# Sorted expert tiles of layer 2: per-expert sets from one table, outputs two tiles behind, finer steps for routing and return

## The chip, the cores and the metric

The kernel runs on one core of a Trainium2 chip. The core has five engines that each work through their own instructions in order: TensorE (PE, matrix products; its weight loads are shown apart as PEld), VectorE (DVE), ScalarE (ACT), GpSimd (POOL) and SyncE (SP, which here only starts transfers). Transfers between the main memory (DRAM) and the on-chip memory are moved by 16 DMA engines; SP, ACT and POOL start them. The metric is the device time of one execution in microseconds, lower is better.

## The reference, cut to what matters

The program is a network of four layers on x[2, 1024, 128]. Each layer adds half a feed-forward part (FFN), an attention, and the same half FFN again:

```
x = x + 0.5 * L2_ffn(layernorm(x));  x = x + L2_attn(x);  x = x + 0.5 * L2_ffn(layernorm(x))
```

Layer 0 has a mixture of 6 experts and a latent attention, layer 1 an FFN that selects columns by an argmax and a compressed, selected and windowed attention, layer 3 a mixture of 8 experts with a small attention in front of it, and between its two FFN parts a gated recurrence (minGRU). Layer 2's FFN is what the change is about. It has 8 experts, and each token uses two of them:

```
logits = x @ router_w                      # [tokens, 8]
gate_vals, gate_idx = top_k(logits, 2);  gate_w = softmax(gate_vals)
h   = gelu(x @ w1[e] + b1[e])              # 128 -> 512
out = h @ w2[e] + b2[e]                    # 512 -> 128
res = x + out
y   = (res - mean(res)) / sqrt(var(res) + 1e-6) * gamma[e] + beta[e]
result = sum over the token's two experts of gate_w * y
```

w1, b1, w2, b2, gamma and beta all belong to the expert. Layer 2's attention has 16 heads of 64, with a norm per head on queries and keys, and a tanh clamp on the scores. Everything is in 32-bit floats.

## The kernel before, in words

x stays on the chip as 16 tiles of 128 tokens; four of them make a quarter q (512 tokens). Work that belongs to another part of the program is cut into pieces and kept in threads: `Ctx.later` (L68) adds a thread, `Ctx.tick` (L71) advances the first `width` threads by one stretch each, up to the next `None`, and `Ctx.need` runs a thread to its end. A main loop calls `tick` once or twice per step, so the pieces land between its own instructions. PE's order is exactly the order of the program text so made. A scheduler orders the other engines, and each engine's queue is in order.

**Layer 2's FFN** (`l2_ffn`, L1316) computes only the two chosen experts of a token, by sorting. It is run twice, before and after layer 2's attention, each time for two halves of 1024 tokens.

- `l2_ffn_prep` (L1196), per quarter: layernorm (`norm_pieces`, transposed by L166), the normed rows stored to DRAM (xd), router (L222), gates and the part of beta (L247, L266, L273).
- `l2_route` (L1223), per half: counts the tokens of each expert with small products (L1246 to L1252), places them (DVE), builds one-hot rows (r_b L1293, r_a) and inverts the list with 16 products (L1303). The result: for each of 23 tiles of 128 sorted rows the token numbers (r_tok) and the tile's expert (r_exi), and for each token where its two rows lie (r_si).
- `l2_ffn` then goes through the tiles in groups of 4 (the last has 3), 46 tiles for two halves. `fetch` gathers a tile's rows (xg, L1331, on POOL), loads its expert number into a register on PE, ACT, DVE and SP (L1332), and starts the transfer of the expert's w1 (256 KB, L1340). `turn` (L1361) transposes a group's rows and copies them out of the accumulator banks as xgT. `hidden` is four products (L1375) and four gelus (L1383), whose bias is picked from a table by the register. `output` is a product of ones with b2 in three bf16 parts (L1393) and four products with w2 (L1402), one tile behind `hidden`. `combine`, per group, adds xg (L1421), takes mean and variance, multiplies by gamma (L1427) and stores the rows to DRAM (yd, L1431). Hidden products of two tiles share one pair of banks. One tick comes with every second tile.
- `l2_back` (L1454), per half, after the half's last store: 16 gathers of 128 rows (yg, L1465), all issued in the first tick of its thread, then for each quarter the scaling and the addition into x (L1470 to L1477).
- `l2_expert_weights` (L1176) loads w2 (2 MB), gamma, and b2, which `three_parts` splits on DVE into three bf16 parts (tag l2f_b, L370). It is called before the second l1_ffn and again near the attention's end.

**Around it.** `l1_ffn` (L679; its second call is the one right before the first tiles) goes through 16 tiles t with one tick each; its steps are L689, L690 (a copy on ACT), L696, L705, L712. `l2_attn` (L1489) goes through 8 groups of four heads. `project` makes a group's queries, keys and values as eight products (L1516, L1520; squares on POOL L1529) and eight turns (L1538, L1542, L1545). The first projection is done in one go before the loop; the others are spread over the 16 steps of the group before. A step has scores (L1586), tanh and exp (L1593, L1594) and mix (L1619). Near its end the last group ticks twice per step. Layer 3's FFN uses `experts` (L280): per quarter eight steps of a hidden product (L290) and an output (L308), with a tick of width 3 per step. Its two calls are named "j" and "k"; in their ticks run layer 3's attention and its norms (xn, nn, zn by L156, L158 and L166; L1737 pq; at; L1784 pp), and after each quarter of "j" the recurrence (xa, L1871, y L1896).

Of the kernel before, what the change touches and what calls it, by code (L numbers as in the profile page):

```python
# [279 lines left out]
def experts(c, pool, rs, w1, w2, b1, func, n, hc, combine, key, b2=None, width=2):  # L280
# [20 lines left out]
    def output(q, e, hT):  # L301
        py = c.long("py").rearrange("p (j d) -> p j d", j=4)
        if b2 is not None:
            rows = b2[:, e * P : (e + 1) * P].unsqueeze(1).to_broadcast([3, 4, P])
            nc.tensor.matmul(py, lhsT=c.ones16[0:3, :], rhs=rows, start=True, stop=False, skip_group_check=True)
        for j in range(4):
            for k in range(hc):
# [4 lines left out]
                    start=(k == 0 and b2 is None),  # L312
                    stop=(k == hc - 1),
                    skip_group_check=b2 is not None,
                )
        return combine(q, e, py)

    last, due = None, deque([[]])

    def step(q=None, e=None):  # L320


        nonlocal last
        now = None if q is None else (q, e, hidden(q, e))
        if last is not None:
            for k, piece in enumerate(output(*last)):
                while len(due) < k + 2:
                    due.append([])
                due[k + 1].append(piece)
        last = now  # L330
        for piece in due.popleft():
            piece()
        if not due:
            due.append([])
        c.tick(width)

    for q in range(NC):
        c.need((key, q))
        for e in range(n):
            step(q, e)  # L340
    step()
    while any(due):
        for piece in due.popleft():
            piece()


def add_gated(c, rs, tile_of, n, done):


    def combine(q, e, py):  # L350
# [5 lines left out]
        return []  # L356
# [322 lines left out]
def l1_ffn(c, w, rs, key, done):  # L679
    nc = c.nc  # L680
    with c.pool("l1f", 2) as pool:
# [54 lines left out]
        for t in range(NT + 5):  # L736
# [4 lines left out]
            if t < NT:  # L741
                av[t] = choose(t)
                if t % 4 == 2 and t // 4 < 3:
                    latent(t // 4 + 1)
            if 0 <= t - 4 < NT:
                aT[t - 4] = output(t - 4, av.pop(t - 4)[1])
            if 0 <= t - 5 < NT:
# [399 lines left out]
def l2_consts(c, pool):  # L1147
    w = {n: c.load(pool, f"l2f_{n}") for n in "router b1 beta".split()}
# [23 lines left out]
def l2_attn_weights(c, pool):  # L1172
    return {n: c.load(pool, f"l2a_{n}") for n in "wq wkv wo norm gq gk".split()}


def l2_expert_weights(c, pool, work):  # L1176
    w = {"w2": c.load(pool, "l2f_w2")}
    w["gamma"] = pool.tile([P, 8, P], F32, tag="l2f_gamma", name="l2f_gamma")
    c.nc.sync.dma_start(
# [964 lines left out]
```

## Time and profile before

| | us |
|---|---|
| median of 13 runs | 3162.29 |
| lowest, highest | 3155.42, 3168.08 |
| profiled execution | 3163.22 |
| span of its trace | 3161.5 |
| mean granted clock of PE | 0.93 |
| PE busy | 2737.2 |
| DVE busy | 2047.7 |

The stages that matter lie in the span as follows. The second l1_ffn runs from 1598.6 to 1685; the first tiles from 1707.06 (their first hidden product) to 1865.7 (last output); layer 2's attention from 1915.96 (first scores) to about 2670; the second tiles from 2687.06 to 2846.86; layer 3 from there to 3161.5.

| window | length | PE busy | DVE busy |
|---|---|---|---|
| second l1_ffn 1599 to 1685 | 86 | 74.93 | 68.61 |
| seam 1685 to 1707 | 22 | 5.46 | 11.78 |
| tiles 1707 to 1768 | 61 | 55.70 | 22.12 |
| first projection 1866 to 1916 | 50 | 21.83 | 33.27 |
| seam 2670 to 2687 | 17 | 2.30 | 10.86 |
| seam 2846 to 2858 | 12 | 3.63 | 7.86 |
| layer 3, 2858 to 2960 | 102 | 95.67 | 83.22 |
| layer 3, 2960 to 3162 | 202 | 181.00 | 123.72 |

How to read the profile: an idle time belongs to the instruction that stands behind it, and the name after the arrow is what released it. Idle time counts only on an engine that the end waits for, which here is mostly PE. A wait for several things is put down to the one that came last by the profile; "issue" means that nothing in the profile explains it. The 40 slices are 79 us each; digits are tenths. The matmul counts of a line in the timeline can be twice those of the code.

### The profile page before, as it was taken

Reading aid. Unit: us, or ns where it says so; the run is one execution under the profiler, and the core shown is the slowest. Engines: PE = TensorE matmul, PEld = TensorE weight load, DVE = VectorE, ACT = ScalarE, POOL = GpSimd, SP = SyncE. Lnnn points to the kernel's source line nnn. Section 1 sums busy time; section 2 is a strip of 40 time slices with the busy share of each in tenths; the row PEclk is TensorE's granted clock in tenths of the full one; section 3 lists DMA queues with packets and bytes.
Section 4 is the critical chain, followed back from the end, with each engine's and each line's share of the span. In section 5 each row is a group of like instructions: output and inputs, shape, how many; then the busy total and the mean of one; then the engine's idle time right before and its main releaser. Section 6 shows DMA issues by size and latency. Waiting matters only on the chain.

```text
span 3161.5 us, 44643 instructions
## 1 busy us (share of the span) xinstructions
PE 2737.2 (87%) x15214; PEld 1563.5 (49%) x15214; DVE 2047.7 (65%) x6398; ACT 1586.2 (50%) x3148; POOL 908.9 (29%) x861
## 2 busy tenths in 40 slices
PE   7899999999898877878876857999989996778989
PEld 5544545444565554444445743333333433776666
DVE  4666556655547768768575358777777786357874
ACT  3355455455433336566523425776766774344543
POOL 0011111111003445444343334443444442332110
PEclk9999999999999759999987879999999998889999
DMA  3000000000000000000013420000000011430000
GB/s 83 1 1 1 1 1 1 1 1 1 12 15 1 1 1 1 1 1 1 28 37 91 112 65 2 1 1 1 1 7 1 1 64 37 112 103 17 1 4 11
DMA packets 48990, 64.87 MB, mean 21 GB/s; under 512 B 9924, under 2 KB 31701, under 8 KB 48124
## 3 DMA queue, kind: packets, MB, share of 16 engines
q1 hardware_dynamic: 38328, 48.74, 5.1%
q0 software_dynamic: 4992, 10.27, 1.7%
q10 hardware_dynamic: 5444, 3.01, 0.4%
q8 instruction: 122, 2.00, 0.3%
q14 instruction: 104, 0.85, 0.1%
HBM read 52.77 MB, written 9.22 MB: 20 GB/s over the span
## 4 chain that ended last, share of the span: by engine, by line
PE 65%; DVE 20%; ACT 5%; issue 4%; POOL 3%; DMA 2%; ACTq 0%; SPq 0%; DVEq 0%; POOLq 0%
PE ps L1586 6%; PE po L1619 6%; PE ph L290 5%; PE ps L492 5%; PE py L308 5%; PE po L534 5%; PE ptp L520 4%; PE ph L1375 3%; PE pr L472 3%; PE py L1402 2%; PE po L1071 2%; PE pt L1059 2%; PE pr L562 1%; PE pqk L1520 1%; ACT pe L1037 1%
## 5 line engine op out<-in xcount | busy, mean ns | idle before, releaser
L1593 ACT ACTIVATE pe<-ps 128x1024 f32<-128x1024 f32 x256 | 249.0, 1021 | 181.7 <-PE ps L1586 129.1
L1586 PE MATMUL ps<-tr 64*128 64x512 f32 x1024 | 269.5, 647 | 1.6 <-ACT pe L1593 1.6
L1619 PE MATMUL po<-pe,v 128*64 128x512 f32 x1024 | 249.9, 609 | 3.7 <-ACT pe L1594 3.7
L505 ACT ACTIVATE pe<-ps,nm 128x512 f32<-128x512 f32 (+3 forms) x384 | 219.3, 577 | 64.3 <-DVE nm L503 60.4
L1594 ACT ACTIVATE pe<-pe 128x2048 f32<-128x2048 f32 x128 | 244.7, 1911 | 4.0
L503 DVE TENSOR_REDUCE nm<-ps 128x2 f32<-128x256 f32 (+1 forms) x192 | 182.6, 951 | 95.1 <-PE ps L501 61.4
L353 DVE SCALAR_TENSOR_TENSOR x<-py,gates,x 128x128 f32<-128x128 f32 x448 | 132.8, 343 | 161.7 <-PE py L308 161.6
L99 ACT COPY pT<-ptp 128x512 f32<-128x512 f32 x192 | 91.9, 479 | 252.2 <-PE ptp L520 252.2
L492 PE MATMUL ps<-kT,qT 64*128 64x512 f32 (+3 forms) x768 | 177.4, 538 | 30.0 <-ACT pe L505 11.4
L1383 ACT ACTIVATE hT<-ph,l2f_b 128x128 f32<-128x128 f32 x368 | 111.4, 366 | 171.0 <-PE ph L1375 161.2
L534 PE MATMUL po<-pT,v 128*64 128x512 f32 (+3 forms) x768 | 166.8, 513 | 0.0
L520 PE MATMUL ptp<-ident,pe 128*128 128x128 f32 x1152 | 162.5, 277 | 0.2 <-ACT rb L570 0.2
L1375 PE MATMUL ph<-xgT,w 128*128 128x128 f32 x736 | 112.7, 301 | 55.2 <-issue 39.6
L1586 PEld LDWEIGHTS ps<-tr 64*128 64x128 f32 x1024 | 92.7, 195 | 125.8 <-issue 90.9
L1619 PEld LDWEIGHTS po<-pe,v 128*64 128x64 f32 x1024 | 62.7, 138 | 179.9 <-issue 152.9
L520 PEld LDWEIGHTS ptp<-ident,pe 128*128 128x128 f32 x1152 | 123.1, 141 | 52.3 <-issue 40.4
L308 PEld LDWEIGHTS py<-l3f_w,hT 128*128 128x128 f32 x1024 | 125.7, 194 | 32.6 <-issue 30.5
L1331 POOL DMA_INDIRECT xg<-xd,r_tok x92 | 87.2, 948 | 189.2 <-issue 95.9
L1606 POOL TENSOR_TENSOR acp<-pe 128x1024 f32<-128x1024 f32 x32 | 76.8, 2401 | 223.3 <-ACT pe L1594 132.9
L1529 POOL TENSOR_TENSOR sq<-raw 128x512 f32<-128x512 f32 x64 | 89.5, 1398 | 164.3 <-DVE raw L1527 107.0
L475 POOL TENSOR_TENSOR qT<-tab 128x512 f32<-128x512 f32 x32 | 40.6, 1269 | 329.4 <-DVE tab L474 184.0
L1045 POOL TENSOR_SCALAR pe<-pe,rs 128x256 f32<-128x256 f32 (+7 forms) x128 | 94.3, 749 | 141.8 <-DVE rs L1042 76.8
(426 smaller groups left out, 6380.7 us busy)
## 6 DMA issues: line engine op xcount, KB each, us to landing
w<-in_l2f_w SPq DMA_DIRECT2D x92, 256.0 KB, 3.4
yd<-y SPq DMA_DIRECT2D x20, 258.0 KB, 3.8
l2f_w<-in_l2f_w SPq DMA_DIRECT2D x2, 2048.0 KB, 8.6
xd<-xn SPq DMA_DIRECT2D x8, 256.0 KB, 2.3
l3f_w<-in_l3f_w SPq DMA_DIRECT2D x2, 1024.0 KB, 4.9
l0f_W<-in_l0f_W SPq DMA_DIRECT2D x2, 768.0 KB, 5.1
xg<-xd,r_tok POOLq DMA_INDIRECT x92, 3.4
l2a_wkv<-in_l2a_wkv SPq DMA_DIRECT2D x1, 1024.0 KB, 5.7
```

The lines of the kernel that those rows point to most:

```text
L290: nc.tensor.matmul(ph[:, a, :], lhsT=w1[:, e, (k + a) * P : (k + a + 1) * P], rhs=rs[q]["xT"], start=True, stop=True)
L308: nc.tensor.matmul(py[:, j, :], lhsT=hT[:, k, j * P : (j + 1) * P], rhs=w2[:, e, k, :], start=(k == 0 and b2 is None), stop=(k == hc - 1), ...
L492: nc.tensor.matmul(ps[:, h, :W], lhsT=u["qT"][r, q0 : q0 + P], rhs=u["kT"][r, gk * 512 : gk * 512 + W], start=True, stop=not diag,)
L503: nc.vector.tensor_reduce(nm, ps[:, :, :W], AX.X, ALU.max, negate=True)
L505: nc.scalar.activation(u["pe", n][:, h, i, :W], ps[:, h, :W], AF.Exp, bias=nm[:, h : h + 1], accum_out=u["rs"][:, n, i, h : h + 1],)
L520: nc.tensor.transpose(pt[:, i * P : (i + 1) * P], u["pe", n][:, h, i, j * P : (j + 1) * P], c.ident)
L534: nc.tensor.matmul(u["po", n][r, lo * P :], lhsT=u["v"][:, BLOCKS[n][1] * 4 + j, cols], rhs=u["pT", n, j][h][:, lo * P :], start=(j == 0), ...
L1375: nc.tensor.matmul(ph[:, a * P : (a + 1) * P], lhsT=wt[:, a * P : (a + 1) * P], rhs=xT[n][:, j * P : (j + 1) * P], start=True, stop=True,)
L1586: nc.tensor.matmul(ps[:, h, :], lhsT=tr[r, 1, p, k * P : (k + 1) * P], rhs=tr[r, 0, p, q * 512 : (q + 1) * 512], start=True, stop=True,)
L1593: nc.scalar.activation(pe[:, j], ps, AF.Tanh, scale=1.0 / 50.0)
L1594: nc.scalar.activation(pe, pe, AF.Exp, scale=50.0 * 0.125)
L1619: nc.tensor.matmul(u["po"][r, :], lhsT=u["v"][:, k, 2 * u["p"] + h, :], rhs=pe[:, j, h, :], start=(k == 0), stop=(k == TB - 1),)
```

## The change

One table in DRAM, `sets[128, 8, 772]`, holds for each expert w1 (512 columns), b1 (4), b2 (128) and gamma (128), the last two repeated on all 128 rows. Four transfers write it when the kernel starts. A tile now fetches two stretches of it: w1 with b1 (264 KB) and b2 with gamma (131 KB), up to six tiles ahead; registers are loaded once per group, on SP and on PE alone. The gelus' bias and the combine's gamma come from the tile's set, and b2 is added on DVE in the combine instead of by a product on PE. `l2_expert_weights` and both calls of `three_parts` are gone.

Outputs come two tiles behind the hidden products (hT has four buffers). A tick comes with every tile, and from tile 12 on two. A half's route is queued right after its gates, and half 0's first gathers and fetches are the tail of its route thread. `l2_back` issues its gathers in four steps with pauses of ticks, and the additions come some ticks after the gathers they need. The attention becomes a class whose first projection runs as thread pieces, so that it falls among half 1's tiles.

The numbers of ticks change: the second l1_ffn has three per t (one before), the last attention group four per step from step 10 on (two before), layer 3's "j" three per step for the first two quarters and two after (one before), "k" two (one before). Ticks now stand on both sides of an output product.

```diff
@@ experts
+            now = (q, e, hidden(q, e))
+            if ticks(q) > 1:
+                c.tick(width)
+            if last is not None:
+                output(*last)
+            if ticks(q) > 2:
+                c.tick(width)
+            last = now
+            c.tick(width)
@@ l1_ffn
+            if ticks > 1:
+                c.tick()
             if 0 <= t - 4 < NT:
                 aT[t - 4] = output(t - 4, av.pop(t - 4)[1])
+            if ticks > 2:
+                c.tick()
@@
-def l2_expert_weights(c, pool, work):
-    w = {"w2": c.load(pool, "l2f_w2")}
...
-    three_parts(c, work, c.load(work, "l2f_b2", rows=3), w["b2"])
+def l2_sets(c, dpool):
+
+    t = dpool.tile([P, 8, 772], F32, tag="sets", name="sets")
+    for cols, src in (
+        (slice(0, 512), c.dram["l2f_w1"]),
+        (slice(512, 516), c.dram["l2f_b1"].rearrange("p (e k) -> p e k", k=4)),
+        (slice(516, 644), c.dram["l2f_b2"].rearrange("o (e d) -> o e d", d=P).to_broadcast([P, 8, P])),
+        (slice(644, 772), c.dram["l2f_gamma"].rearrange("o (e d) -> o e d", d=P).to_broadcast([P, 8, P])),
+    ):
+        c.nc.sync.dma_start(out=t[:, :, cols], in_=src)
+    return t
@@ l2_ffn_prep
-    return [begin] + norm[:i] + [store] + norm[i:] + gates + [end]
+    return [begin] + norm[:i] + [store] + norm[i:] + gates[:1] + [chosen] + gates[1:]
@@ class L2Experts
+        halves[0]["then"] = [self.gather, self.fetch, self.fetch, None, self.gather] + [self.fetch] * 2
...
+    def fetch(self):
+
+        k = self.fetched
+        n, j = self.tiles[k]
+        if j == 0:
+            self.register[n] = self.load(n, ("SP",))
+        t = self.set[k] = {}
+        for name, cols, bufs in (("w1b1", slice(0, 516), 7), ("b2g", slice(516, 772), 10)):
+            t[name] = self.pool.tile([P, cols.stop - cols.start], F32, tag=name, name=name, bufs=bufs)
+            src = self.sets[:, bass.ds(self.register[n][j], 1), cols].rearrange("p e f -> p (e f)")
+            self.nc.sync.dma_start(out=t[name], in_=src)
+        self.fetched += 1
...
+        while self.gathered < min(self.tiles[k][0] + 3, len(self.groups)) and self.routed(self.gathered):
+            self.gather()
+        while self.fetched < min(k + 6, len(self.tiles)) and self.routed(self.tiles[self.fetched][0]):
+            self.fetch()
...
+                for a in range(4):
+                    b1 = t[:, 512 + a : 513 + a]
+                    nc.scalar.activation(hT[:, a, :], ph[:, a * P : (a + 1) * P], AF.Gelu, bias=b1)
...
+                nc.vector.tensor_add(res[:, 0:m, :], py[:, 0:m, :], self.xg[n][:, 0:m, :])
+                sets = [self.set.pop(k + j)["b2g"] for j in range(m)]
+                for j in range(m):
+                    nc.vector.tensor_add(res[:, j, :], res[:, j, :], sets[j][:, 0:P])
...
+            for k, (n, j) in enumerate(tiles):
+                self.ahead(k)
+                if k == 0:
+                    turn(0)
+                queue.append((k, n, j, hidden(k, n, j)))
+                c.tick()
+                if len(queue) > 2:
+                    output(*queue.popleft())
+                if j == 2 and n + 1 < len(groups):
+                    if n + 1 == self.gathered:
+                        self.ahead(k + 1)
+                    turn(n + 1)
+                if k >= 12:
+                    c.tick()
@@ l2_back
-    return [partial(fetch, 0), partial(fetch, 1), None, None, None, partial(add, 0), None, partial(add, 1), None]
+    pieces = [None] * 5
+    for piece in (partial(fetch, 0, 0), partial(fetch, 0, 1), partial(fetch, 1, 0)):
+        pieces += [piece, None, None, None]
+    return pieces + [partial(add, 0), partial(fetch, 1, 1)] + [None] * 5 + [partial(add, 1), None]
@@ class L2Attention
+    def first(self, a):
+
+        if a == 0:
+            self.ready, self.products, self.turns = self.project(0, 0)
+        pieces = []
+        for p in self.products[4 * a : 4 * a + 4]:
+            pieces += [p, None]
+        if a == 1:
+            pieces += [None, None, None]
+            for p in self.turns:
+                pieces += [p, None]
+        return pieces
...
+                    if n + 1 == len(groups) and s >= 10:
+                        c.tick()
@@
-        l1_ffn(c, w1, r[5], "f", prep1)
-    l2_ffn(c, w2, we, keep2, h1, follow("h", partial(l2_attn_prep, c, wa, r[6])))
+        l1_ffn(c, w1, r[5], "f", prep1, 3)
...
+    e1.run(prep_attn)
...
-    l2_ffn(c, w2, we, keep2, h2, both_places)
-    l3_ffn(c, w3, r[3], "j", recur)
-    l3_ffn(c, w3, r[4], "k", store)
+    e2[0].run(both_places)
+    l3_ffn(c, w3, r[3], "j", recur, lambda q: 3 if q < 2 else 2)
+    l3_ffn(c, w3, r[4], "k", store, lambda q: 2)
```

## The prediction

> **What bounds the kernel now.** I read the page first (busy shares, slices), then the idle stretches of TensorE (PE) in its timeline, then busy time by stage, then the waits.
>
> The page says that PE is busy 87% of the span and carries 65% of the chain that ended last; VectorE (DVE) carries 20%. The tenths of PE show where the missing 13% lies: slices of 79 us, and the dips at slices 21 to 25 and 34 to 37 are the two stages of sorted tiles, where the only real DMA traffic lies too.
>
> ```profile
> span 3161.5 us, 44643 instructions
> PE 2737.2 (87%) x15214; PEld 1563.5 (49%) x15214; DVE 2047.7 (65%) x6398; ACT 1586.2 (50%) x3148; POOL 908.9 (29%) x861
> PE   7899999999898877878876857999989996778989
> DMA  3000000000000000000013420000000011430000
> PE 65%; DVE 20%; ACT 5%; issue 4%; POOL 3%; DMA 2%; ACTq 0%; SPq 0%; DVEq 0%; POOLq 0%
> ```
>
> The timeline of PE names each stop: start, duration, line, and in brackets the idle time and its releaser. Four are over 13 us. L696 opens the second l1_ffn. L1303 and then L1375 stand behind the routing of half 1. The 15.67 us before L1375 is called "issue", but the xgT copy on DVE that this product needs runs at 1833.77, behind the additions of l2_back (L1470, L1477). L1542 is the first turn of layer 2's attention, waiting for eight products' norms.
>
> ```profile
> 1598.59 2.04 PE L696 MATMUL pr<-l1f_m2mb,lr 65*128 65x512 f32 x2 [13.60 <-ACT lr L690]
> ...
> 1775.16 0.82 PE L1303 MATMUL pt<-r_b,r_a 128*128 128x48 bf16 x16 [7.17 <-DVE r_b L1293]
> 1780.06 2.05 PE L1375 MATMUL ph<-xgT,w 128*128 128x128 f32 x8 [4.08 <-issue]
> ...
> 1834.55 2.05 PE L1375 MATMUL ph<-xgT,w 128*128 128x128 f32 x8 [15.67 <-issue]
> ...
> 1907.16 1.97 PE L1542 MATMUL ppt<-ident,raw 128*128 128x128 f32 x8 [17.88 <-DVE raw L1538]
> ```
>
> Busy time by stage (window, its length, then busy us of PE, PEld, DVE, ACT, POOL, granted clock, DMA share, GB/s): undisturbed tiles keep PE at 97% with DVE a third busy; between them PE stands and DVE works alone, and the granted clock falls to 0.55-0.69.
>
> ```profile
> 1685.00:1707.00 22.00, 5.46 (x50) 3.86 (x49) 11.78 (x56) 3.34 (x7) 7.02 (x8) 0.63 0.44 137
> 1768.00:1780.00 12.00, 0.82 (x16) 0.69 (x16) 7.20 (x23) 0.00 (x0) 2.23 (x3) 0.55 0.39 115
> 1780.00:1819.00 39.00, 37.95 (x271) 33.88 (x271) 12.34 (x60) 19.48 (x62) 27.55 (x30) 0.92 0.57 138
> 1819.00:1835.00 16.00, 0.45 (x2) 0.48 (x3) 11.29 (x61) 0.09 (x1) 7.00 (x8) 0.65 0.35 98
> 1866.00:1916.00 50.00, 21.83 (x82) 14.68 (x80) 33.27 (x95) 0.00 (x0) 23.79 (x24) 0.69 0.10 25
> ```
>
> Layer 3, by contrast, stops little, and its stops are chains of norms: nn waits longest. A short stop leaves the next product at its usual 1.88 us, a longer one slows it.
>
> ```profile
> 2946.39 0.82 PE L166 MATMUL pt<-ident,nn 128*128 128x128 f32 x4 [1.31 <-ACT nn L158]
> 2947.05 1.88 PE L290 MATMUL ph<-xT,l3f_w 128*128 128x512 f32 x4
> ...
> 2985.87 1.12 PE L166 MATMUL pt<-ident,nn 128*128 128x128 f32 x4 [3.46 <-ACT nn L158]
> 2986.78 3.62 PE L290 MATMUL ph<-xT,l3f_w 128*128 128x512 f32 x4
> 2990.20 2.41 PE L308 MATMUL py<-l3f_w,hT 128*128 128x128 f32 x16
> ```
>
> **The change part by part.** The profiled execution took 3163.22 us, 1.7 more than its span; that is 0.03% above the median, so I subtract from the span, add 1.7, and take off 1.
>
> *Second l1_ffn to the first tile (1583 to 1707.06).* L690's copy stood on ScalarE behind the transfer of b2 and three_parts on DVE. Both go; PE still waits about a microsecond for that copy, so 13.6 becomes 1: -12.6. Three ticks per t instead of one put the norms, gates and route of half 0 among l1_ffn's steps. That takes away the waits of the seam, 3.97 (gates), 7.26 (r_b) and 5.50 (first gathers), 16.7 in all. The same chains must still run, under l1_ffn's remaining PE work (75 us busy in 86, DVE 69): their latencies are 7 to 11 us each where DVE is shared. I give back 11: net -18. Ends: -8 (nearly all the seam's waits come back) and -25.
>
> *First tiles to the first scores (1707.06 to 1915.96, 208.9).* PE's work afterwards, at undisturbed durations: 46 tiles at 1.09 hidden and 1.09 output, 100; twelve turns at 0.44, 5; every second hidden waits for the gelus of its pair of banks as before, 23 x 0.35, 8; prep, gates and route of what is left, about 6; the first projection, now thread pieces, 8 products at 1.49 (1917.88 to 1919.37) and 8 turns at 0.63, 17. Sum 136. The b2 product (0.155 start to start, 46 times, 7) is gone from it. Its place is taken by 46 additions of 128x128 on DVE, estimated at 0.25 from the neighbouring 0.34 of a scalar_tensor_tensor of that shape: 11.5. DVE's 100 us of before become 112 in about 150, so it isn't the bound on average, but l2_back, the norms and the projection all fall into tiles 31 to 46. I allow 14 us of stalls: up to 5 at half 1's route (chain 7.3, cover about 9), the rest there. 150 against 208.9: -59. Ends: -68 (half the stalls) and -40 (the projection's norms uncovered).
>
> What hides the rest: register loads, now one per group on SP and PE, leave ACT and DVE, worth nothing on PE's path outside the 4.08 already counted. SP gets two transfers per tile instead of one: at the static 0.33 to 0.43 plus a share of a register load, 1.1 to 1.6 us per tile of 2.9. Behind each y store (L1431), which waits for DVE, now stand the sets of later tiles; they lead by six tiles, 17 us. The table's four transfers at the kernel's start stand behind layer 0's loads on SP (its last ends at 22 us) and before nothing that layer 0 needs: nothing, and at most their landing, some 10 us, if a layer-0 load is delayed. POOL issues the same 23 x 2 gathers of 1.25; those of l2_back come in fours and let others pass.
>
> *Attention.* The second three_parts stood in PE's way for 3.28 at 2593.86: -3. Ends -7 and +2; the groups between are unchanged.
>
> *End of attention to the second tiles (2640 to 2687.06).* PE is busy 22.3 of 47. Four ticks per step bring gates and route between the last scores; of the waits (4.28, 4.45, 7.50, 6.00) I take 15 of 22 as covered. Ends -20 and -8.
>
> *Second tiles (2687.06 to 2846.86, 159.8).* As above without the projection: 46 tiles 100, turns 5, pairs 8, route 3, and the layer-3 prep of two quarters 11-13, of which 5.5 comes from after the tiles: 129. Its chains are packed at two ticks per tile, some 2.4 us apart where they take 4 to 9: 14 of stalls. 143: -17. Ends -30 and 0.
>
> *Layer 3 (2846.86 to 3161.5, 314.6).* PE's order shows what comes closer together. After the last output PE now runs 7 expert steps of 3.5 us before nn of the last two quarters, instead of 10 and a wait of 7.5. But nn needs the y store (7 us from its issue to the first gather), 16 gathers at 1.25, 3.4 to land, the additions 3 and a norm of 5 or more: 38 to 40 us. So 14 us of waiting come back where 7.5 and 3 steps stood; about even for the seam by itself. Then pq to at has one py (1.78) between where the chain takes 4.3; pp to zn has 3.5 to 5.8 where it takes 9 (3008.29 to 3017.45); y to nn 3.5 to 7 where it takes 8 or more (21 with 15 of cover before). I count 20 for the packed quarters, 7 for each of three later ones, and 2.2 for each restart after a long wait (3.62+2.41 against 1.88+1.95 above), twelve in all. Together 68 against 31 of waits and 9 of restarts before, less the 5.5 moved: +22. Ends -5 (the chains overlap) and +60 (the latencies are those of a crowded DVE).
>
> Sum: -18 -59 -3 -15 -17 +22 = -90. 3161.5 - 90 + 1.7 - 1 = 3072.
>
> **The rivals.**
>
> *Transfers bind the tiles.* The new 131 KB per tile on 2.41 us is 58 GB/s on top of 138, so the measured share of 0.57 becomes 0.57 x 196/138 = 0.81: not full, but a set that arrives late stops a hidden product. For it: gathers, stores and sets peak together. Against it: sets lead by six tiles. At 0.4 us per tile x 92 = 37: 3109. The Trainium skill, "DMA: Bandwidth & Descriptors", section "Issuing engines are not separate DMA queues", says that all queues share the same 16 engines, so that the gathers on POOL feel SP's traffic; its specifications give a ceiling of 435 GB/s, by which 196 would leave more than half free and the sum would stay at 3072. I go by the measured share.
>
> *Packed pieces stall fully.* Layer 3 at +60 and the second tiles at 0: 3072 + 38 + 17 = 3127. For it: the covers counted above. Against it: while PE waits, DVE catches up, and DVE is 61% busy after 2960.
>
> *The projection isn't hidden.* Its turns wait for eight products, POOL squares and DVE sums, queued in order behind l2_back and the combines; then the 28 us idle of 1866 to 1916 stays: 3100.
>
> *Slower: the sync queue.* A y store that waits on a late combine holds all sets behind it. It decides once a combine comes over 17 - 3.8 = 13 us late; then each of 24 groups pays the excess, and from 3.75 us each the gain of 90 is gone: 5 us gives 24 x 5 = 120, so 3190. For it: DVE also works in order, and one of its waits on a gather was 6.91 (bvar). Against it: DVE is a third busy in undisturbed tiles, and the gathers are now issued well ahead of the additions.
>
> **How the numbers follow.** The forecast has 0.56, transfers 0.12, packed pieces 0.12, the open projection 0.11, the sync queue 0.09. Within 0.2% of before (6 us, about what a measurement of this kernel tells from no change) lies only the space between packed pieces and sync queue: 0.03, taken in equal parts from both. So faster 0.89, same 0.03, slower 0.08. The forecast's own ends by stage add to -155 and +6, but hardly all fall together; half of that either way is 3030 to 3120. The range takes in the three rivals on the fast side: 3020 to 3130.
>
> **What the profile afterwards would show.** L696 after a wait of about 1 instead of 13.6; no wait over 6 us before the route's product; the first scores 150 us after the first hidden; no "issue" wait of 15 us between groups; DMA share near 0.8 in the middle of the tiles; a wait of 10 to 16 us before the first nn after the tiles, and waits of 2 to 5 before at, zn and nn in layer 3. The prediction is wrong if hidden products wait for w1b1, if the sync queue's stores hold sets, or if layer 3 from the last output takes over 350 us instead of 337.

## The result and the profile after

The changed kernel takes 3208.30 us (median; 3204.68 to 3214.48) against 3161.02 us for the kernel before, measured beside it: a ratio of 1.0147, with a 95% interval of 1.0137 to 1.0158. It is 47 us slower. The forecast was 3072 us, 90 faster, with a range up to 3130: it is wrong in sign, and the time lies outside the range. The profiled execution of after took 3211.02 us with a span of 3209.1.

The page of after: the busy times, the tenths of TensorE (PE) and of the DMA engines in 40 slices of 80 us, and the shares of the chain that ended last.

```profile
span 3209.1 us, 43956 instructions
PE 2729.5 (85%) x15122; PEld 1568.9 (49%) x15122; DVE 2061.1 (64%) x6472; ACT 1579.1 (49%) x3145; POOL 907.5 (28%) x861
PE   7999999999898878878868678999989987576679
DMA  4000000000000000000105510000000115400000
PE 6%; DVE 4%; POOL 1%; ACT 1%; issue 1%; DMA 0%; DVEq 0%; ACTq 0%; POOLq 0%
```

PE has 8 us less work than before (2729.5 against 2737.2) in 48 us more of span, so taken as a whole the loss is waiting. The dip at slice 21 is the second l1_ffn, the one at slice 23 the stop in the first stage of tiles, the one at slice 35 that in the second. New are slices 36 to 39, layer 3: 7, 6, 6 and 7, where before had 7, 8, 9 and 8. (The shares of the chain add up to 13% here, so I read nothing from that line.)

The stages, from PE's timeline, in us. "Second l1_ffn" runs from the first to the end of the last product of lr with m2mb (L679, in before L696), the first product of each of its 16 tiles; "seam" from there to the first hidden product of the tiles, with the last steps of l1_ffn in it; "tiles" from there to the end of the last output product. So the borders differ a little from those ahead of the prediction, where the seam begins at 1685 and the second tiles end one product later. The numbers of before and after are from their profiled executions.

| stage | before | after | forecast of the difference | difference |
|---|---|---|---|---|
| start of second l1_ffn (its first product of lr at) | 1598.6 | 1587.0 | -12.6 | -11.6 |
| second l1_ffn and seam | 65.4 + 43.1 | 87.1 + 38.0 | -5.4 | +16.6 |
| first tiles | 158.8 | 162.8 | | +4.0 |
| from there to the first scores | 50.1 | 0 | -59 with the tiles | -50.1 |
| attention, first to last scores | 738.2 | 764.8 | -3 | +26.6 |
| to the second tiles | 32.9 | 24.1 | -15 | -8.8 |
| second tiles | 158.9 | 166.0 | -17 | +7.1 |
| layer 3 to the last product | 311.0 | 375.4 | +22 | +64.4 |

The differences add to 48.2. (Single entries move between profiles of one kernel: the start of the second l1_ffn by 9 us in one of the kernels below, 1586.9 and 1596.0, and the attention of after took 764.8, 764.9 and 771.8 in three profiles.) Four places carry the failure: layer 3, attention, the second l1_ffn, and the tiles, which were to become much shorter and did not.

The timeline of PE in after, with start, duration, line, tile and, in brackets, the idle time and what ended it:

```profile
1587.04 1.10 PE L679 MATMUL pr<-l1f_m2mb,lr 65*128 65x512 f32 x2 [0.82 <-ACT lr L673]
...
1637.21 1.51 PE L166 MATMUL pt<-ident,xn 128*128 128x128 f32 x4 [9.36 <-ACT xn L158]
...
1665.77 1.01 PE L166 MATMUL pt<-ident,xn 128*128 128x128 f32 x3 [7.35 <-ACT xn L158]
...
1687.01 0.82 PE L1297 MATMUL pt<-r_b,r_a 128*128 128x48 bf16 x16 [5.65 <-DVE r_b L1287]
...
1817.31 0.48 PE L166 MATMUL pt<-ident,xn 128*128 128x128 f32 x1 [22.19 <-ACT xn L158]
...
1899.09 1.22 PE L1528 MATMUL pv<-l2a_wkv,xT 128*128 128x256 f32 x2 [6.19 <-DVE v L1529]
...
1913.21 1.22 PE L1528 MATMUL pv<-l2a_wkv,xT 128*128 128x256 f32 x2 [5.62 <-DVE v L1529]
...
2770.06 2.04 PE L1395 MATMUL ph<-xgT,w1b 128*128 128x128 f32 x8 [21.77 <-issue]
```

The copy of lr no longer waits for b2's transfer: 13.60 became 0.82, as forecast. But the norms that were put between the steps of l1_ffn wait there (9.36 and 7.35), and each stage of tiles has one stop of 22 us.

Busy time by stage of after (window, its length, busy us of PE, PEld, DVE, ACT, POOL, granted clock, DMA share, GB/s):

```profile
1712.00:1795.00 83.00, 74.23 (x620) 70.92 (x620) 43.11 (x199) 43.96 (x146) 29.58 (x31) 0.95 0.72 193
1795.00:1818.00 23.00, 0.59 (x3) 0.18 (x1) 11.41 (x69) 1.24 (x4) 14.34 (x15) 0.60 0.23 55
1818.00:1875.00 57.00, 47.02 (x296) 42.19 (x298) 45.33 (x157) 16.09 (x52) 8.32 (x8) 0.86 0.28 74
2748.00:2770.00 22.00, 0.30 (x3) 0.10 (x1) 10.73 (x54) 0.63 (x3) 14.12 (x15) 0.59 0.26 64
2830.00:3209.00 379.00, 291.52 (x1544) 210.42 (x1542) 209.91 (x1109) 129.12 (x182) 34.47 (x52) 0.89 0.03 8
```

The undisturbed tiles (first row) run at 0.72 of the DMA engines and 193 GB/s, where the forecast had worked out 0.81 and 196, and in the whole program hidden products waited for a set once, for 0.9 us. Between turns a tile takes 2.12 us there (1.89 and 2.34 by turns from one hidden product to the next) against 2.40 before (2.24 and 2.57). So the part of the change that the diff is mostly about, sets from one table and outputs two behind, does what was forecast; no run separates the two. In the two stops of 22 us no engine is full: DVE is busy for half of them, POOL for 14 us, PE for less than 1.

Layer 3 of after, in PE's timeline:

```profile
2849.47 3.76 PE L305 MATMUL py<-l3f_w,hT 128*128 128x128 f32 x16 [9.33 <-DVE nh L110]
...
2928.45 1.11 PE L166 MATMUL pt<-ident,nn 128*128 128x128 f32 x4 [13.44 <-ACT nn L158]
2929.36 3.58 PE L290 MATMUL ph<-xT,l3f_w 128*128 128x512 f32 x4
...
2996.64 1.11 PE L166 MATMUL pt<-ident,nn 128*128 128x128 f32 x4 [8.10 <-ACT nn L158]
2997.55 3.62 PE L290 MATMUL ph<-xT,l3f_w 128*128 128x512 f32 x4
...
3048.72 1.11 PE L166 MATMUL pt<-ident,nn 128*128 128x128 f32 x4 [8.14 <-ACT nn L158]
```

From the last output on, before waits five times for nn: 0.21, 1.31, 3.46, 5.27 and 5.33. After waits six times: 2.73, 3.25, 13.44, 8.10, 8.14 and 8.14, and behind the last four the next ph takes 2.8 to 3.6 instead of 1.88.

### The profile page after: what moved, and what is told of

Its sections match the earlier page's. It is cut to its first block, busy times and chain, and to the rows that moved or that the text cites. A ratio compares the mean times of both kernels' runs of the same rounds, so it can differ in the third digit from the quotient of the medians.

```text
span 3209.1 us, 43956 instructions
## 1 busy us (share of the span) xinstructions
PE 2729.5 (85%) x15122; PEld 1568.9 (49%) x15122; DVE 2061.1 (64%) x6472; ACT 1579.1 (49%) x3145; POOL 907.5 (28%) x861
## 5 line engine op out<-in xcount | busy, mean ns | idle before, releaser
L475 PE MATMUL ps<-kT,qT 64*128 64x512 f32 (+3 forms) x768 | 177.8, 539 | 30.0 <-ACT pe L488 11.3
L1404 ACT ACTIVATE hT<-ph,w1b 128x128 f32<-128x128 f32 x368 | 105.1, 369 | 145.0 <-issue 111.8
L1395 PE MATMUL ph<-xgT,w1b 128*128 128x128 f32 x736 | 111.2, 300 | 41.5 <-issue 25.5
L305 PE MATMUL py<-l3f_w,hT 128*128 128x128 f32 x1024 | 132.0, 285 | 10.6 <-DVE nh L110 9.3
L294 ACT ACTIVATE hT<-ph 128x1024 f32<-128x1024 f32 x64 | 65.5, 1023 | 144.0 <-PE ph L290 144.0
```

The source lines that it names most:

```text
L305: nc.tensor.matmul(py[:, j, :], lhsT=hT[:, k, j * P : (j + 1) * P], rhs=w2[:, e, k, :], start=(k == 0), stop=(k == hc - 1),)
L475: nc.tensor.matmul(ps[:, h, :W], lhsT=u["qT"][r, q0 : q0 + P], rhs=u["kT"][r, gk * 512 : gk * 512 + W], start=True, stop=not diag,)
L1395: nc.tensor.matmul(ph[:, a * P : (a + 1) * P], lhsT=t[:, a * P : (a + 1) * P], rhs=xT[n][:, j * P : (j + 1) * P], start=True, stop=True,)
```

## The experiments

Theory: layer 3's ticks (three per step in the first two quarters, two after) pack a quarter's chain of norms so closely that PE waits for every link, and this is the largest loss. Rivals: the loss in layer 3 comes from the return that reaches into it from the last tiles (the seam); or it comes from elsewhere, from the ticks in the second l1_ffn, the early projection, or the split return. The runs were made on five chips. On two of them the kernel before took 3224 to 3226 us and on the others 3162 to 3170, so a ratio is always to runs of before on the same chip, and times are subtracted within one chip only. In the profiles from those two chips ACT, DVE and SP have waits whose releaser is named "remote", and the stages of tiles are 10 us and more longer than in the same kernels elsewhere; profiles from the other chips have no such wait.

**Layer 3 as before.** One tick per step, and the return of the last half (its name is 21) in the old order:

```diff
-    l3_ffn(c, w3, r[3], "j", recur, lambda q: 3 if q < 2 else 2)
-    l3_ffn(c, w3, r[4], "k", store, lambda q: 2)
+    l3_ffn(c, w3, r[3], "j", recur, lambda q: 1)
+    l3_ffn(c, w3, r[4], "k", store, lambda q: 1)
@@ l2_back
+    if h["name"] in ('21',):
+        gathers = [partial(fetch, a, k) for a in range(2) for k in range(2)]
+        return gathers + [None] * 3 + [partial(add, 0), None, partial(add, 1), None]
```

> The changed kernel with layer 3 undone alone: one tick per expert step in both FFN calls, and the last half's return with its gathers in one piece as before. In the changed kernel layer 3 took 375 us from the last tile's output to the end, against 311 before. Theory (the packing of layer 3's chains costs it): 311 to 320 again, 3145 to 3155 in all. Rival (the additions of the last half stand too early in DVE's queue, and that alone costs the seam): most of the 64 us stay, 3185 to 3200.

Measured: 3183.10 us, 0.9871 [0.9827, 0.9916] of before, with 308.0 in layer 3. With this undone alone, the kernel is faster than before. As this chip is one of the two with "remote" waits, the run was made again on another, beside after and before:

> The changed kernel again, on the chip of the runs beside it, since the kernel before took 3224 us on the chip of the first experiments against 3161 on the first one. If the chip makes no difference to the comparison: 1.5% over before. If the changed kernel suffers less from what slows that chip: level with before or faster.

> The kernel before with a profile on this chip. If what slows a chip lies in the gathers and transfers, its two tile stages are longer than 158.8 and 158.9 us and engines show waits named remote; if it lies in TensorE's clock, all stages are longer alike.

> Layer 3 undone alone, beside the changed kernel on one chip. Theory (packing of layer 3's chains): 60 to 67 us less than the changed kernel. Rival (the seam alone): 15 to 25 us less.

Measured: before 3168.37 us (3167.32 in its own profiled execution), after 3214.16, 1.0144 [1.0097, 1.0191], and with layer 3 as before 3148.80, 0.9936 [0.9911, 0.996]. So packing layer 3 costs 65 us, more than the whole loss of 46: without it the rest of the change gains 20. Busy time from the last output to the end in these two profiles (columns as above), first after, then layer 3 as before:

```profile
2833.00:3205.00 372.00, 288.14 (x1544) 206.69 (x1542) 209.53 (x1107) 129.00 (x182) 34.80 (x52) 0.91 0.03 7
```

```profile
2833.00:3142.00 309.00, 275.75 (x1542) 202.68 (x1541) 201.60 (x1105) 130.85 (x184) 35.03 (x52) 0.94 0.03 8
```

The same products (1544 and 1542 in the traces) take 63 us more. PE idles 372 - 288.1 = 83.9 against 33.3, so 50.6 of it is waiting, and 12.4 is PE itself, slower at a lower granted clock (0.91 against 0.94) after the waits. The waits of PE for nn over the whole program, in the same order (us in total, times, longest):

```profile
PE pt L166 <- ACT nn L158: 48.2, 8, 13.5
```

```profile
PE pt L166 <- ACT nn L158: 20.4, 6, 5.4
```

That is 28 of the 50. By the timelines of the two, waits for zn add 13 (six of 1.5 to 3.6 against one of 1.55) and for y 6 (2.15, 2.70 and 2.87 against 1.49).

**Three ticks in the first quarter only.** This tells the seam and the first packed quarter from the later ones; the return of the last half stays in the new order.

```diff
-    l3_ffn(c, w3, r[3], "j", recur, lambda q: 3 if q < 2 else 2)
-    l3_ffn(c, w3, r[4], "k", store, lambda q: 2)
+    l3_ffn(c, w3, r[3], "j", recur, lambda q: 3 if q < 1 else 1)
+    l3_ffn(c, w3, r[4], "k", store, lambda q: 1)
```

> The changed kernel with its three ticks per step kept for the first quarter of layer 3's first FFN, and one tick everywhere after. Layer 3 took 372 us in the changed kernel and 310 with it undone. If the first quarters after the tiles cost most of it, as the prediction had it (14 at the seam and 20 for the packed quarters, 7 for each of the other three): 340 to 350 in layer 3. If the later quarters cost most: 315 to 325.

Measured: 3151.88 us, 0.9949 [0.9932, 0.9965], against 0.9936 for layer 3 wholly as before, with overlapping intervals. The stage takes 313.3 us against 309.7. PE's timeline of this kernel at the seam:

```profile
2849.99 3.75 PE L305 MATMUL py<-l3f_w,hT 128*128 128x128 f32 x16 [9.69 <-DVE nh L110]
...
2872.58 0.82 PE L166 MATMUL pt<-ident,nn 128*128 128x128 f32 x4 [2.74 <-ACT nn L158]
2876.66 1.12 PE L166 MATMUL pt<-ident,nn 128*128 128x128 f32 x4 [3.26 <-ACT nn L158]
```

The wait of 9.7 at the seam is there with one tick too (9.59 at 2852.77), and packing the first quarter costs under 4 us. So the seam rival falls: some 60 of the 65 us come with the ticks of the later quarters, of which the second of "j" is the other one with three ticks. PE's waits in the three kernels, by quarter, summed from the timelines (us, borders by the count of hidden products):

| kernel | j 1 | j 2 | j 3 | j 4 | k 1 | k 2 | k 3, 4 |
|---|---|---|---|---|---|---|---|
| layer 3 as before | 11.3 | 4.2 | 1.8 | 3.7 | 6.8 | 5.3 | 0 |
| three ticks in the first quarter | 17.0 | 0.4 | 2.9 | 3.8 | 6.8 | 5.4 | 0 |
| after | 16.9 | 25.1 | 12.1 | 13.7 | 14.0 | 1.6 | 0 |

(After here is its run beside layer 3 as before.) Of the 50 us more, 21 come in the second quarter of "j", 10 in each of the next two, 7 in the first of "k" and 6 in the first of "j"; the second of "k" waits 4 less.

**The other parts, with layer 3 as before.** Each of the next runs leaves layer 3 as before and undoes more. The second l1_ffn with one tick:

```diff
-        l1_ffn(c, w1, r[5], "f", prep1, 3)
+        l1_ffn(c, w1, r[5], "f", prep1, 1)
```

> As the run with layer 3 undone, but with one tick per step in the second selected FFN, as before the change. Theory (norms and route packed three ticks to a step make TensorE wait inside that FFN: 87 us instead of 65, for 5 us won at the seam): 12 to 20 us less than the run with layer 3 undone. Rival (the same chains then run at the seam, uncovered): within 5 us of it, either way.

Measured: 3172.09 us, 0.9838 [0.9798, 0.9878]: 11 us less than with layer 3 alone undone on that chip, with overlapping runs. From the start of the second l1_ffn to the first hidden product it takes 108.4 us instead of 134.9, and the tiles then are 12 longer.

The first projection after the tiles again, as before, instead of as pieces among them:

```diff
-        first = [lambda: c.later(("first", q), attn.first(q))] if q < 2 else []
+        first = []
@@ L2Attention.run
                 c.need((self.key, a))
-                c.need(("first", a))
-            ready = self.ready
+            ready, *work = self.project(0, 0)
+            for piece in work[0] + work[1]:
+                piece()
```

> As the run with layer 3 undone, but the first projection of the attention is made in one go after the tiles, as before the change. Theory (its place among the tiles is what shortened the way from the first tile to the first scores by 46 us): 20 to 30 us more than the run with layer 3 undone. Rival (its pieces crowd DVE in the tiles and pay back what they save): within 8 us of it.

Measured: 3181.85 us, 0.9872 [0.983, 0.9914], against 3183.10 with the projection among the tiles: no difference. Yet the stages move a lot: tiles 151.4 instead of 175.2, to the first scores 48.9 instead of 0, attention 741.3 instead of 768.2. The projection's 50 us are hidden, and come back as 24 in the tiles and 27 in the attention.

Both undone, on the chip of after:

> Layer 3, the ticks of the second selected FFN and the place of the first projection undone together; what stays of the change is the table with its sets, the outputs two tiles behind, the ticks in the tiles and at the attention's end, and the split return. Theory (the table and the finer tile steps are worth something, the three packings are not): 5 to 15 us less than with layer 3 undone alone. Rival (the projection among the tiles is worth its 20 us once the FFN's ticks no longer stand before it): 10 to 20 us more.

Measured: 3137.41 us, 0.9899 [0.9875, 0.9923], which is 11.4 less than with layer 3 alone undone (runs of 3136.11 to 3144.18 against 3146.61 to 3150.08). The stages of the kernels of that chip, from PE's timeline:

| kernel | l1_ffn + seam | first tiles | to scores | attention | to tiles | second tiles | layer 3 |
|---|---|---|---|---|---|---|---|
| before | 65.4 + 42.5 | 159.3 | 50.1 | 739.4 | 33.2 | 160.6 | 310.2 |
| after | 87.1 + 38.0 | 162.7 | 0 | 764.9 | 24.1 | 165.9 | 371.7 |
| layer 3 as before | 87.0 + 38.0 | 161.5 | 0 | 769.5 | 24.1 | 165.9 | 309.7 |
| and l1_ffn, projection | 64.4 + 44.0 | 150.2 | 49.0 | 736.8 | 24.0 | 165.9 | 308.0 |

The ticks of l1_ffn cost 125.0 - 108.4 = 16.6 us up to the first hidden product. Between there and the end of the attention the kernel with both undone takes 936.0 - 931.0 = 5 us more. The two agree with the 11.4 of the times. Whether the 5 belong to the projection isn't shown: on the other chip the ticks undone alone made the tiles 12 longer, and the projection undone alone changed nothing.

**The stop in the tiles.** What the stop of 22 us waits for is in the timelines of POOL and DVE of after. POOL, whole gathers of the return (L1476):

```profile
2737.72 0.94 POOL L1476 DMA_INDIRECT yg<-yd,r_si  x1 [4.84 <-DMA b2g<-sets]
2738.97 0.94 POOL L1476 DMA_INDIRECT yg<-yd,r_si  x1 [0.30 <-issue]
...
2761.65 0.94 POOL L1476 DMA_INDIRECT yg<-yd,r_si  x1 [0.30 <-issue]
```

DVE at the same place:

```profile
2750.87 0.29 DVE L1481 COPY bvar<-yg 128x8 f32<-128x8 f32 x1 [11.96 <-DMA yg<-yd,r_si]
...
2764.25 0.17 DVE L1481 COPY bvar<-yg 128x8 f32<-128x8 f32 x1 [7.86 <-DMA yg<-yd,r_si]
2765.21 0.68 DVE L1429 TENSOR_TENSOR res<-py,xg 128x512 f32<-128x512 f32 x1
...
2769.28 0.68 DVE L97 COPY xgT<-pt 128x512 f32<-128x512 f32 x1
```

The first gather starts 7.3 us after the store of the half's last rows is issued on SP (2730.39). Sixteen of them and four gathers of later tiles, at 1.25 each, keep POOL until 2762.6. DVE works in order: bvar, the first copy of each addition, waits for its gathers (11.96 and 7.86), and behind it stand the combine and the copy xgT that PE's next hidden product needs. PE's "issue" is this wait. The additions were put some ticks after the gathers, but with two ticks in a tile of 2.12 us a tick is about 1 us, and the nine from the first gathers to the first addition do not hold the 13 us to the landing at 2750.9 and the five to the second not the 13 after that. In the first tiles it is the same, with the norm xn of quarter 0 (22.19) behind the second bvar.

The next kernels hold the additions back: the gathers first, more ticks before each addition, and the copy bvar tied to a recent value of DVE's other work, which enters it times zero, so that it is not ordered earlier.

```diff
@@ l2_back
-    return pieces + [partial(add, 0), partial(fetch, 1, 1)] + [None] * 5 + [partial(add, 1), None]
+    return pieces + [partial(fetch, 1, 1)] + [None] * 4 + [partial(add, 0)] + [None] * 10 + [partial(add, 1), None]
@@ add
-        nc.vector.tensor_copy(var, yg[a][:, :, :, P])
+        if c.mark is None:
+            nc.vector.tensor_copy(var, yg[a][:, :, :, P])
+        else:
+            nc.vector.scalar_tensor_tensor(var, c.mark, 0.0, yg[a][:, :, :, P], ALU.mult, ALU.add)
```

The mark is the mean of the latest combine in the tiles and, in the first form, a part of the attention's acc.

> As the run with layer 3 undone, and the additions of the return are held back in DVE's queue: the first instruction of an addition also reads a value of a later tile group (or of a later attention group), multiplied by zero, so that it can't stand before it, and it is issued some ticks later. Theory (DVE's queue stands on an addition whose gathers have not landed, with the combine and the copy of the turned rows behind it): the two waits of 22 us of TensorE in the tiles and the 12 us of waits in the first attention group go, 30 to 45 us less than the run with layer 3 undone. Rival (DVE or the transfers are simply overloaded there, the queue's order doesn't matter): within 10 us of it.

Measured, with layer 3 alone as before: 3199.38 us, 0.9919 [0.9893, 0.9945], 16 us more than without the hold. A miss: the tiles did not get shorter (177.6 and 178.0) and the attention got longer. This was on a chip with "remote" waits, so it was tried again on one without, now with l1_ffn and projection as before too (the third of the next runs has the projection among the tiles). On that chip without the hold, and with it:

> The kernel with the three packings undone (layer 3, the second selected FFN, the projection) again, as the reference of the runs beside it: 1% under before.

> The three packings undone, and the additions of the return held back as in the earlier run of that kind: behind a later combine in DVE's queue, and some ticks later. In the first such run, on a chip where engines showed waits named remote, this made the kernel 16 us slower. Theory (each of the two tile stages loses 20 us because PE or DVE comes to the return before its 16 gathers, at 1.25 us each, have landed): 20 to 35 us less than the reference. Rival (the work behind the return is late in any case, and the wait only moves to the projection and to layer 3): within 8 us.

> As the run with the additions held back, but with the first projection among the tiles. Theory (with the return out of the way the projection's pieces find room beside the last tiles): 10 to 25 us less than with the projection after the tiles. Rival (they come too late and take the time of the attention's start instead): within 8 us.

Measured: 3138.55, 0.991 [0.9891, 0.9928] without; 3135.00, 0.9893 [0.9877, 0.991] with the hold; 3129.41, 0.9877 [0.986, 0.9893] with the hold and the projection among the tiles. The tiles fall from 149.1 and 164.8 to 135.1 and 153.7, but the attention rises from 736.6 to 757.5: what the hold takes from the tiles, most of it, comes back there, and the runs with and without it overlap. The projection among the tiles gains 5.6 in this setting.

So the mark was left in the tiles alone; layer 3 and l1_ffn are as before, and in the first of the two the projection is too:

> The three packings undone and the additions held back in the tiles alone; in the attention they stand where the change puts them. In the run that held them in both, the two tile stages took 135 and 154 us instead of 149 and 165, but the way from the first scores to the last 757 us instead of 737. Theory (the 21 us in the attention come from half 1's additions held behind an attention group's sums; with the projection after the tiles its idle time covers them): tiles 135 and 154, attention 737, 15 to 22 us less than the run that held both, that is about 1.7% under before. Rival (whatever is late after the tiles is paid in the attention): attention 750 or more, within 6 us of it.

> The same with the first projection among the tiles, so that nothing stands between the tiles and the scores that half 1's return could lie beside. Theory (that is why the attention took 765 to 770 us in every kernel with the projection among the tiles and 737 to 741 with it behind them): attention 760 or more, and 10 us or more over the run with the projection after the tiles. Rival (the projection gains once both waits are gone): at least level with it.

Measured on a chip with "remote" waits: 3175.55, 0.9838 [0.9812, 0.9863], and with the projection among the tiles 3180.93, 0.986 [0.9834, 0.9885]. The attention takes 736.6 and 765.0, as the two theories had it, but the second kernel is not 10 us slower, and the tiles of the first, 170.6 and 177.6, are far from 135 and 154 on this chip. Here the early projection loses 5.4, where it lost 1.3 in the first pair and gained 5.6 in the one before: what it is worth has no steady sign, and the intervals of each pair overlap.

The first of the two once more, beside after, on a chip without such waits:

> The three packings undone and the additions held back in the tiles alone, once more: the first run of it fell on a chip where the kernel before takes 3226 us and engines show waits named remote. On a chip where before takes 3160 to 3170: tile stages of 135 and 154 us, attention 737, 1.6 to 1.9% under before. If it falls on a chip of the slower kind again: 1.6% under before, as there.

> The changed kernel beside it. On a chip where before takes 3160 to 3170: 1.4 to 1.5% over before, as in two earlier measurements. On a chip of the slower kind, where the runs with layer 3 undone were 1.3% under before: by the same 65 us of layer 3, about 0.7% over before.

Measured: before 3161.73, after 3213.67, 1.0150 [1.0126, 1.0174], the held kernel 3117.66, 0.9851 [0.9829, 0.9872]: it beats both, 44 us under before and 96 under after. (The gain is a little less than the 1.6 to 1.9% expected. Without the hold the ratio was 0.9899 and 0.991 on other chips; the two were not measured side by side.) Its tiles take 136.4 and 153.8, its attention 743.1, its layer 3 309.7. PE's timeline of it where after stopped for 22.19, and in the second stage, where after stopped for 21.77:

```profile
1802.48 1.11 PE L167 MATMUL pt<-ident,xn 128*128 128x128 f32 x4 [9.13 <-ACT xn L159]
...
1820.03 1.07 PE L167 MATMUL pt<-ident,xn 128*128 128x128 f32 x4 [4.19 <-ACT xn L159]
...
2766.35 1.12 PE L167 MATMUL pt<-ident,nn 128*128 128x128 f32 x4 [10.41 <-ACT nn L159]
```

(Its lines are one further down than after's.) Of the 22.19, 9.13 and 4.19 are left, for norms of the same line; in place of the 21.77 stand 10.41 for a norm and, before it, 4.12 for gathered rows.

## Why the prediction was wrong

- *Layer 3, +22.* This is the largest error: +64 in the profiled execution, +61.5 between the profiles of one chip. The step that failed is the count "20 for the packed quarters, 7 for each of three later ones". The mechanism, chains packed closer than they take, was right, and the order of PE's products showed it; the sizes were not. The three later quarters waited 12.1, 13.7 and 14.0, so 40 instead of 21: each has a wait of about 8 for nn alone and 2 to 4 for y and zn beside it. Seam and packed quarters together waited 42 instead of the 34 of the sum, where the first one lost no more than 6 by being packed and the second 21. With the last 1.6, waits were 83 where the sum had 55 (its listed terms give 67 with the 12 of restarts, not 68), against 33 with layer 3 as before, and the restarts grew by 12.4 where it had 3 (12 against 9). The wait of "10 to 16 us before the first nn" came as 9.33 before an output product, with 2.73 and 3.25 before nn. The forecast's own upper end, +60, was the value. The condition "takes over 350 us" came true at 375.
- *Attention, -3, and first tiles to first scores, -59.* By the traces they are one thing. The first scores do come with the last output (50.1 became 0), but half 1's return, which lay beside the projection before, now lies in the attention: DVE stands at bvar for 12.47 with the copy of v behind it, and PE waits 6.19 and 5.62 for v (shown above). In the first 100 us of the attention PE's waits add to 25.7, 16.3 of them for v; in before they are 9.3 and 1.4. The timeline of DVE in after:

```profile
1893.72 0.17 DVE L1481 COPY bvar<-yg 128x8 f32<-128x8 f32 x1 [12.47 <-DMA yg<-yd,r_si]
...
1898.62 0.41 DVE L1529 COPY v<-pv 128x256 f32<-128x256 f32 x1
```

  Of the -46 of the one, 27 come back in the other. With the additions held back in the attention too, and the projection among the tiles, the attention was no shorter (770.0), so that moving the return out of its first group alone does not mend it. The projection undone, the time does not change (3181.85 against 3183.10). The step that failed is "the groups between are unchanged": the sum had moved the projection, and not what then met the attention.
- *Second l1_ffn to the first tile, -18.* The 12.6 of lr came as forecast. The 11 given back for the chains under l1_ffn were 33 (16.6 + 16.7): by the borders of the table l1_ffn grew by 21.7 and the seam shrank by 5.1, so that the stage was +16.6 instead of -5.4. PE waited 9.36 and 7.35 for xn: a norm's latency of that order is a wait wherever PE's order puts its product, and moving it in front of work that could have covered it costs. Undone alone, it was worth 11 us on the one chip where that was run.
- *Tiles, -17 in the second stage.* Undisturbed tiles fell to 2.12 us each, as counted (2.18). The 14 us of stalls allowed were one stop of 22 and what lies around it: +7 instead of -17. That "those of l2_back come in fours and let others pass" did not hold: twelve came in one row and four gathers of tiles between them and the last four, and an addition waited for them at the head of DVE's queue. The prediction had seen this wait (6.91 for bvar) and set against it that the gathers are issued well ahead of the additions; nine and five ticks were not enough. With the additions held in the tiles and the three packings undone the stages are 136.4 and 153.8.
- *End of attention, -15.* -8.8, within the ends given.
- *The rivals.* Transfers do not bind: 0.72 of the DMA engines, one wait of 0.9 for w1b. (131 KB on 2.41 us are 54 GB/s rather than the prediction's 58, so its share should have been 0.79.) On the sync queue transfers of sets did wait for y of the combines, 19 times and 137 us in all, but that reached no hidden product beyond the 0.9. "Packed pieces stall fully" had the two prices nearly right (+60 in layer 3, 0 in the second tiles; +64 and +7 came), and was still 81 us too low, since it kept the other terms. "The projection isn't hidden" had the idle time in the wrong place. The rival that ended slower named the wrong queue: what held was DVE's order behind POOL's gathers, with one stop of 22 us per stage and not at each group.
- *The sum.* The terms -90 and the measured +48 differ by 138: layer 3 42, attention 30, second tiles 24, l1_ffn and seam 22, first tiles and gap 13, end of attention 6, start 1. Every error has the same sign. What they share, as I read them (no run tested it as one): each price was that of a link on its own, and each piece moved earlier met others that were moved earlier too, on a DVE that works in order.

## What to carry to other kernels

Placing a chain's pieces closer together shortens nothing when PE must then wait for each link: for every link, set the other work that stands between producer and consumer in PE's order against the latency measured in that stage; what the work doesn't cover is a wait, and it counts for every link. Moving a piece to an earlier place pays only if what lay beside it before still has cover. An addition that waits for gathers belongs behind the work it could block on its engine, not a fixed number of ticks after the gathers: sixteen gathers at 1.25 us, as here, are 20 us on POOL whatever the ticks are.

## What the runs showed of the hardware

The restart after a wait was much as the trace before had it: in after, beside the waits of 8 to 13 us for nn, the next ph took 2.8 to 3.6 us, and beside those of 2.15 and 2.70 for y it took 1.88. The Trainium skill, "TensorE: Matmul & The Clock Gate", "Part 1: The HAM clock gate", has the clock fall after an idle window of about 3.4 us. These waits lie on both sides of it, but shorter ones slowed PE too: behind waits of 3.25 for nn and 3.03 for zn the granted clock was 0.50 (2876 to 2881 and 2947.4 to 2956 us), where it was 1.00 behind the 2.15 and 2.70, and behind one of 1.83 for xa it was 0.67 (2969 to 2973). So in this trace the length of the last wait alone does not tell which product is slow. What I had not expected is the sum: 12.4 us in layer 3 alone.

Two chips ran the kernel before 2% slower than the others. Profiles of kernels run there (before itself was not profiled there) have waits named "remote" on ACT and DVE, most of them on SP too. On one of them the waits of ACT and DVE in the kernel with layer 3 as before read (us in total, times, longest):

```profile
ACT xgT L99 <- remote: 24.0, 2, 18.6
ACT hT L1404 <- remote: 16.7, 2, 15.6
ACT aT L705 <- remote: 13.3, 1, 13.3
DVE x L713 <- remote: 8.7, 1, 8.7
```

What they are was not found; no experiment was made for it.
